# The last superchunk of a macaron block, finished token tile by token tile

## The chip, the cores and the metric

The kernel runs on one core of a Trainium2 chip. The core has TensorE (PE, with its weight loads shown as PEld), VectorE (DVE), ScalarE (ACT), GpSimd (POOL) and the queues that issue transfers, SyncE (SP) and POOL's own. The metric is the device time of one execution in microseconds.

## The reference

The input is x of 8 sequences of 1024 tokens with 256 channels, float32. Three blocks follow each other, each added to its input:

```
x = x + 0.5 * ffn(layernorm(x))
x = x + mamba(layernorm(x))
x = x + 0.5 * ffn(layernorm(x))

ffn(x):    xq = fp4(x);  h = silu(xq @ fp4(w_gate).T) * (xq @ fp4(w_up).T)      # 704 wide
           return fp4(h) @ fp4(w_down).T
fp4(v):    blocks of 16 along the last axis: scale = max(max|v| / 6, 1e-12),
           v / scale rounded to the grid 0, .5, 1, 1.5, 2, 3, 4, 6, times scale
mamba(x):  xi, z = split(norm(x) @ in_proj)            # 512 each
           xi = silu(causal depthwise conv of 4(xi));  dt, B, C = split(xi @ x_proj)
           delta = softplus(dt @ dt_proj + b)
           for each of 16 states n, along time:  h_n = exp(-A_n delta) h_n + delta xi B_n
           y = sum over n of h_n * C_n  +  D * xi
           return (y * silu(z)) @ out_proj
```

## The kernel before

Each sequence is cut into two superchunks of 512 tokens, 16 in all (0 to 15). A superchunk goes through five stages, written as generators: `stage_f1` (first feed-forward), `stage_m1` (up to delta and its product with the convolved input), `stage_z` (the gate silu(z), written to DRAM as `szd`), `scan` (the 16 states) and `stage_out` (gating, out projection, second feed-forward). `spread` gives each yield of each generator a due time, so that stages of neighbouring superchunks are written down interleaved. Inner channels lie on partitions in four chunks (`dc` 0 to 3), tokens along the free axis; the out projection and the feed-forwards work on token tiles of 128 (four in a superchunk).

The order that the program keeps is not the written one. At the end `set_order` builds a graph of all instructions with costs (`price`) and lags, makes eight plans forward and backward over the whole program, and fixes the order of each engine's instructions to the plan with the least estimated end. A change in one place can so move instructions elsewhere.

In `scan`, state k of a superchunk goes through `scan_step` (L802: the recurrence on DVE, one instruction for each inner chunk) and `times_c` (L810: h times C, nearly always on POOL, two inner chunks at a time), and is then added to y in DRAM by a transfer that accumulates (L835, POOL's queue). There are two such sums, for even and odd states. For the last superchunk (`s >= S - KE`, superchunk 15) the last two states, 14 and 15, are not sent to DRAM: `times_c` takes one inner chunk at a time there (state 14 on POOL, state 15 on DVE), and the two h are kept in `last_h`. `load_y` fetches the sum of the other states: one load by SP (L753) and one accumulating load by POOL's queue (L754).

In `stage_out` of the last superchunk, for each inner chunk, DVE adds both kept h to y (L768), the gate's chunk is loaded into `o_sz` (one buffer, L770), and DVE multiplies (L771). Only with all four inner chunks done can a token tile's out projection be complete: four matmuls (L776), which contract over the inner chunks, and the addition to x (L777). The second feed-forward follows: `ln_stats` (bn_stats on DVE, small operations on ACT, a power on POOL), normalization on ACT (L541) into `f_xn`, `quant` (L459 to L469: block maximum on DVE, scale `q_sc` on POOL, reciprocal on DVE, product, square on ACT into PSUM, two rounding passes on DVE, product), transposes on PE (L547), copy to `f_xt` (L549). This is done for two tiles at a time (`XN = 2`). Then for each tile `ffn_h` (gate and up matmuls L559, tanh L562, products L563 and L564 into `f_h`), `quant` of `f_h`, and `ffn_o` (transposes L571 and L575, copies into `f_ht`, down projection L579, addition L580). The products of `quant` of x are on POOL, for `f_h` of the last superchunk's tiles the first is on DVE and the second on POOL. For earlier superchunks both are on POOL, and `f_ht` has one buffer.

PSUM tiles of `stage_out` of the last superchunk are taken in turn from three small pools: `PSM[5] = (1, 0, 1, 0, 2)`, with two, one and one buffers in pools 0, 1 and 2.

Of the kernel before, what the change touches and what calls it, by code (L numbers as in the profile page):

```python
# [20 lines left out]
P = 128  # L21
T = 512
# [14 lines left out]
KS = 1  # L37
KE = 1
# [4 lines left out]
BUFS = {  # L43
    'accd': 4, 'bcol': 2, 'big': 2, 'bu': 8, 'carry': 2, 'cbc': 2, 'cd': 4, 'da': 4, 'delta': 2,
# [3 lines left out]
}  # L48
T_O = 0.1
XN = 2  # L50
QN = 768
DG = 2
HXP = (0, 1, 2, 3)
YG = 2
# [7 lines left out]
ND = DI // P  # L62
# [293 lines left out]
def macaron(ctx: ExitStack, tc: tile.TileContext, x_in, norm_w, norm_b, in_w, conv_w,  # L356
            conv_b, xp_w, dt_w, dt_b, a_log, d_par, out_w, w_gate, w_up, w_down, out):
    nc = tc.nc
    NB, L, _ = x_in.shape
    chunks = []  # L360
    for b in range(NB):
        t = 0
# [24 lines left out]
    sb, psq, psb, dr = Pool(sb), Pool(psq), Pool(psb), Pool(dr)  # L387
    pools = [Pool(q) for q in pools]

    def pst(shape, name):  # L390
        turn[kind[0]] += 1
        i = PSM[kind[0]][turn[kind[0]] % len(PSM[kind[0]])]
        t = pools[i].tile([P, 512], F32, tag=f"ps{i}", name=name)
        n = 1
        for k in shape[1:]:
            n *= k
        v = t[: shape[0], :n]
        if len(shape) == 3:
# [16 lines left out]
    def eng(what):  # L415
        return getattr(nc, ENG[what])
# [9 lines left out]
    outw = cload([P, ND, DM], out_w.rearrange("(c p) n -> p c n", p=P), "outw")  # L426
# [104 lines left out]
        return [(nm[:, i : i + 1], y[:, i : i + 1]) for i in range(nt)]  # L531


    def ffn_x(x4, nt, stats, t0):
        n = min(XN, nt - t0)
        if len(stats) == t0:
            stats += ln_stats(x4, t0, t0 + n, EPS)
        xn = sb.tile([P, XN, DM], F32, tag="xn", bufs=BUFS["xn"], name="f_xn")[:, :n]
        for j in range(n):
            b, r = stats[t0 + j]  # L540
            nc.scalar.activation(xn[:, j, :], x4[:, t0 + j, :], AF.Identity, bias=b, scale=r)  # L541
        quant(xn.rearrange("p a b -> p (a b)"), n * DM, 1e-12, eng('xx'), eng('xq'))
        for j0 in range(0, n, 2):
            pt = pst([P, 2, 2 * P], "f_pt")
            for j in range(2):
                for c in range(2):
                    nc.tensor.transpose(pt[:, c, j * P : (j + 1) * P], xn[:, j0 + j, c * P : (c + 1) * P], ident)  # L547
            xt = sb.tile([P, 2, 2 * P], F32, tag="xt", bufs=BUFS["xt"], name="f_xt")
            nc.scalar.activation(xt, pt, AF.Copy)  # L549
            for j in range(2):  # L550
                yield xt[:, :, j * P : (j + 1) * P]

    def ffn_h(xt, h2):
        for hf in range(2):
# [24 lines left out]
            nc.tensor.matmul(po, ht[:, k, :], wdn[:, k, :], start=(k == 0), stop=(k == NF - 1))  # L579
        nc.vector.scalar_tensor_tensor(x4[:, t, :], po, 0.25, x4[:, t, :], ALU.mult, ALU.add)  # L580

    def ffn(x4, nt, muls, fine):

        stats = [] if fine else ln_stats(x4, 0, nt, EPS)
        yield
        xts = list(ffn_x(x4, nt, stats, 0))
        yield
        hs = []
        hts = [None] * nt
        if fine:  # L590
            hts = []
            for t in range(0, nt, 2):
                two = sb.tile([P, ND * T], F32, tag="h", bufs=BUFS["h"], name="f_ht")[:, : 2 * NF * P]
                two = two.rearrange("p (t k n) -> p t k n", t=2, k=NF)
                hts += [two[:, 0], two[:, 1]]
        for t in range(nt):
            h = sb.tile([P, FF], F32, tag="h2", bufs=BUFS["h2"], name="f_h2")
            ffn_h(xts[t], h)
            yield
            if t + 1 == len(xts) < nt:  # L600
                xts += ffn_x(x4, nt, stats, len(xts))
# [12 lines left out]
    x1d, accd, szd, cd = {}, {}, {}, {}  # L614
    duT, delta, bcol = {}, {}, {}
# [132 lines left out]
    y_of, last_h = {}, {}  # L748
# [8 lines left out]
    def stage_out(s):  # L757
        n = chunks[s][2]
        nt = n // P
        muls = (eng('hx'), eng('hq')) if s < S - ENDV else (nc.vector, nc.vector)  # L760
        x4 = sb.tile([P, NT, DM], F32, tag="x4", bufs=BUFS["x4"], name="x4b")
        nc.sync.dma_start(x4[:, :nt], x1d[s][:, :nt])
        y = y_of.pop(s) if s in y_of else load_y(s)
        yg = 1 if s in last_h else YG
        for dc in range(0, ND, yg):
            if s in last_h:
                for j in range(2):
                    nc.vector.tensor_tensor(y[:, dc, :], y[:, dc, :], last_h[s][j][:, dc, :], ALU.add)  # L768
            sz = sb.tile([P, YG, T], F32, tag="sz", bufs=BUFS["sz"], name="o_sz")[:, :yg, :n]
            nc.sync.dma_start(sz, szd[s][:, dc : dc + yg, :n])  # L770
            (eng('y') if s < S - KE else nc.vector).tensor_tensor(y[:, dc : dc + yg, :], y[:, dc : dc + yg, :], sz, ALU.mult)  # L771
        yield
        for t in range(nt):
            po = pst([P, DM], "o_po")
            for dc in range(ND):
                nc.tensor.matmul(po, y[:, dc, t * P : (t + 1) * P], outw[:, dc, :], start=(dc == 0), stop=(dc == ND - 1))  # L776
# [26 lines left out]
    def times_c(s, k, h, cbc):  # L803
        n = chunks[s][2]
        c_v = CE[S - 1 - s] if S - 1 - s < len(CE) else 0
        cm = 1 if s >= S - KE and k >= NS - 2 else CM
        for dc in range(0, ND, cm):
            hv = h[:, dc : dc + cm, :]
            eng_c = nc.vector if dc < c_v or cm < CM and k % 2 else nc.gpsimd
            eng_c.tensor_tensor(hv, hv, cbc.unsqueeze(1).to_broadcast([P, cm, n]), ALU.mult)  # L810

    def scan(s):
        n = chunks[s][2]
        if chunks[s][1] == 0:

            carry[chunks[s][0]] = sb.tile([P, NS, ND], F32, tag="carry", bufs=BUFS["carry"], name="s_carry")
        for k in range(0, NS, 2):
            cbc = sb.tile([P, 2, T], F32, tag="cbc", bufs=BUFS["cbc"], name="s_cbc")[:, :, :n]
            nc.sync.dma_start(cbc, cd[s][0:1, k * n : (k + 2) * n].rearrange("o (a t) -> o a t", a=2)
                              .partition_broadcast(P))  # L820
            if s >= S - KE and k == NS - 2:
                y_of[s] = load_y(s)
            last = s >= S - KE and k == NS - 2
            for j in range(2):
                h = sb.tile([P, ND, T], F32, tag="h", bufs=BUFS["h"], name="s_h")[:, :, :n]
                scan_step(s, k + j, h)
                if chunks[s][1] + n < L:
                    nc.scalar.activation(carry[chunks[s][0]][:, k + j, :], h[:, :, n - 1], AF.Copy)  # L828
                times_c(s, k + j, h, cbc[:, j, :])
                if last:  # L830
                    last_h.setdefault(s, []).append(h)
                elif k + j == 1:
                    nc.sync.dma_start(accd[s][1, :, :, :n], h)
                else:
                    nc.gpsimd.dma_start(accd[s][j, :, :, :n], h, accum_op=ALU.add)  # L835
                yield
# [12 lines left out]
    t0 = m1 = 0.0  # L849
    for s in range(S):  # L850
# [42 lines left out]
```

## Time and profile before

| | |
|---|---|
| median of three runs | 2534.21 us (2523.82 to 2535.66) |
| the profiled execution | 2536.37 us, span 2534.4 us |
| instructions | 33625 |
| DVE busy | 2184.4 us (86%) |
| POOL busy | 2177.2 us (86%) |
| ACT busy | 2146.9 us (85%) |
| granted TensorE clock, mean | 0.985 |

The page of a profile gives busy times over the span, the span in slices, the transfers, the chain of waits that ended last, and the costliest groups of instructions. In a group's line stands: line of the kernel, engine, operation, output and inputs by their names, shapes, count, busy time and the mean of one in ns, then the idle time before it and what ended that. In a timeline: start and duration in us, then the same, with the idle time in brackets. In the busy times by stretch: the stretch, its length, the busy time of each engine with the number of instructions, the granted clock, the share of the transfer engines and GB/s. The last superchunk's end is short against the span: its last scan instruction ends at 2448.2 of 2534.4 us.

### The profile page before, as it was taken

The numbers are of one execution on the slowest core, as the hardware profiler recorded it, in microseconds if no ns is written. First come the engines' busy times: TensorE is split into PE (matmuls) and PEld (weight loads), VectorE is DVE, ScalarE is ACT, GpSimd is POOL, SyncE is SP. The second block draws the span as 40 slices with busy tenths as digits, with TensorE's granted clock in tenths as the row PEclk, the third lists the DMA queues.
The fourth block names the chain that finished last, engine by engine and source line by source line (L and its number), as shares of the span: only waits on it lengthen the run. The fifth ranks groups of instructions, "written<-read, shape, count | busy, mean of one in ns | idle before, by whom it ended". The sixth has DMA issues, their size and how long they took to land.

```text
span 2534.4 us, 33625 instructions
## 1 busy us (share of the span) xinstructions
PE 2344.9 (93%) x10980; PEld 1591.6 (63%) x10980; DVE 2184.4 (86%) x3082; ACT 2146.9 (85%) x3952; POOL 2177.2 (86%) x1556
## 2 busy tenths in 40 slices
PE   5989898999999999999999999999999999888876
PEld 3555565766666666666666666666666666655544
DVE  7568797998989899898989899898989989878885
ACT  4489787998989988999888989898989988999842
POOL 4359798899989999899998999899997999899952
PEclk9989999999999999999999999999999999999998
DMA  3049779699888988789897998889896988999950
GB/s 90 9 117 207 194 163 223 163 186 238 166 197 195 218 202 189 205 171 239 176 219 173 201 221 176 211 173 221 195 202 181 189 225 175 216 235 211 232 127 17
DMA packets 113647, 465.57 MB, mean 184 GB/s; under 512 B 14592, under 2 KB 32896, under 8 KB 76864
## 3 DMA queue, kind: packets, MB, share of 16 engines
q0 software_dynamic: 36576, 266.35, 56.3%
q1 hardware_dynamic: 76896, 197.08, 24.2%
q8 instruction: 86, 1.41, 0.2%
q14 instruction: 89, 0.73, 0.1%
HBM read 146.19 MB, written 317.19 MB: 183 GB/s over the span
## 4 chain that ended last, share of the span: by engine, by line
POOL 36%; PE 27%; issue 11%; DVE 9%; ACT 9%; DMA 8%; POOLq 0%; SPq 0%; DVEq 0%; ACTq 0%
POOL s_h L810 20%; PE f_pg L559 4%; PE f_pu L559 4%; PE f_po L579 4%; PE s_pb L800 4%; POOL accd L835 4%; DVE s_h L802 4%; DMA accd<-s_h 3%; PE m_pc L682 3%; POOL f_h L462 3%; POOL f_h L469 3%; ACT s_bu L793 2%; ACT s_da L797 2%; POOL f_xn L469 2%; POOL o_y L771 2%
## 5 line engine op out<-in xcount | busy, mean ns | idle before, releaser
L810 POOL TENSOR_TENSOR s_h<-s_h,s_cbc 128x1024 f32<-128x1024 f32 x512 | 1281.8, 2596 | 51.7 <-ACT s_carry L828 27.0
L797 ACT ACTIVATE s_da<-m_delta,an 128x512 f32<-128x512 f32 x1024 | 714.5, 715 | 44.5 <-DVE s_h L802 42.8
L793 ACT ACTIVATE s_bu<-m_duT,m_bc 128x512 f32<-128x512 f32 x1024 | 693.4, 715 | 15.6 <-PE s_pb L800 14.1
L800 PEld LDWEIGHTS s_pb<-ident,s_bu 128*128 128x128 f32 x4096 | 498.0, 142 | 330.2 <-issue 123.4
L800 PE MATMUL s_pb<-ident,s_bu 128*128 128x128 f32 x4096 | 639.2, 277 | 50.9 <-DVE s_h L802 47.4
L802 DVE TENSOR_TENSOR_SCAN s_h<-s_da,s_carry,s_pb 128x512 f32<-128x512 f32 x512 | 636.5, 1265 | 16.5 <-PE s_pb L800 13.3
L802 DVE TENSOR_TENSOR_SCAN s_h<-s_da,s_pb 128x512 f32<-128x512 f32 x512 | 604.4, 1206 | 35.0 <-PE s_pb L800 21.1
L579 PE MATMUL f_po<-wdn,f_ht 128*128 128x256 f32 x1536 | 393.1, 387 | 11.5 <-ACT f_ht L576 6.8
L559 PE MATMUL f_pg<-wg,f_xt 128*128 128x352 f32 x1024 | 370.5, 473 | 13.7 <-ACT f_xt L549 6.2
L559 PE MATMUL f_pu<-wu,f_xt 128*128 128x352 f32 x1024 | 365.6, 468 | 14.1 <-DVE f_h L563 8.4
L579 PEld LDWEIGHTS f_po<-wdn,f_ht 128*128 128x128 f32 x1536 | 276.1, 192 | 73.3 <-ACT f_ht L576 17.0
L835 POOL DMA_DIRECT2D accd<-s_h x238 | 230.7, 969 | 31.8 <-POOL s_h L810 24.1
L559 PEld LDWEIGHTS f_pu<-wu,f_xt 128*128 128x128 f32 x1024 | 182.6, 193 | 115.7 <-issue 34.5
L682 PE MATMUL m_pc<-m_xp,cdg 128*128 128x512 f32 x512 | 252.7, 595 | 2.4 <-ACT m_car L679 2.4
L469 POOL TENSOR_TENSOR f_h<-f_h,q_sc 128x704 f32<-128x704 f32 x128 | 206.5, 1616 | 54.9 <-DVE f_h L468 50.5
L559 PEld LDWEIGHTS f_pg<-wg,f_xt 128*128 128x128 f32 x1024 | 180.3, 195 | 93.4 <-issue 15.1
L462 POOL TENSOR_TENSOR f_h<-f_h,q_rc 128x704 f32<-128x704 f32 x120 | 184.9, 1541 | 22.7 <-DVE q_rc L461 21.9
L563 DVE SCALAR_TENSOR_TENSOR f_h<-f_h,f_pg 128x352 f32<-128x352 f32 x256 | 128.7, 506 | 86.4 <-ACT f_h L562 85.5
L460 POOL TENSOR_SCALAR q_sc<-q_mx 128x44 f32<-128x44 f32 (+2 forms) x198 | 98.0, 497 | 88.5 <-DVE q_mx L459 83.8
L564 DVE TENSOR_TENSOR f_h<-f_h,f_pu 128x352 f32<-128x352 f32 x256 | 129.5, 507 | 41.6 <-PE f_pu L559 39.9
L562 ACT ACTIVATE f_h<-f_pg 128x352 f32<-128x352 f32 x256 | 115.6, 456 | 48.1 <-PE f_pg L559 46.6
L776 PE MATMUL o_po<-outw,o_y 128*128 128x256 f32 x512 | 129.3, 387 | 5.5 <-POOL o_y L771 2.9
(110 smaller groups left out, 3299.6 us busy)
## 6 DMA issues: line engine op xcount, KB each, us to landing
accd<-s_h POOLq DMA_DIRECT2D x238, 1024.0 KB, 9.7
s_cbc<-cd SPq DMA_DIRECT2D x128, 512.0 KB, 5.6
accd<-m_ud SPq DMA_DIRECT2D x64, 256.0 KB, 9.3
accd<-s_h SPq DMA_DIRECT2D x16, 1024.0 KB, 6.8
szd<-m_tz SPq DMA_DIRECT2D x64, 256.0 KB, 6.8
o_y<-accd SPq DMA_DIRECT2D x16, 1024.0 KB, 9.9
o_y<-accd POOLq DMA_DIRECT2D x16, 1024.0 KB, 9.1
o_sz<-szd SPq DMA_DIRECT2D x30, 512.0 KB, 5.1
```

What stands on the lines that cost most here:

```text
L462: mul0.tensor_tensor(vb, vb, rc.unsqueeze(2).to_broadcast([P, g, BLK]), ALU.mult)
L469: mul1.tensor_tensor(vb, vb, sc.unsqueeze(2).to_broadcast([P, g, BLK]), ALU.mult)
L559: nc.tensor.matmul(dst, xt[:, c, :], w[:, c, hf * FH : (hf + 1) * FH], start=(c == 0), stop=(c == 1))
L564: nc.vector.tensor_tensor(hh, hh, pu, ALU.mult)
L579: nc.tensor.matmul(po, ht[:, k, :], wdn[:, k, :], start=(k == 0), stop=(k == NF - 1))
L682: nc.tensor.matmul(pc, cdg[:, dc, k, :], xp[:, k : k + n], start=(k == 0), stop=(k == KC - 1))
L793: nc.scalar.activation(b, duT[s][t], AF.Copy, scale=bcol[s][:, t, k : k + 1])
L797: nc.scalar.activation(da, delta[s][dc], AF.Exp, scale=an[:, dc, k : k + 1])
L800: nc.tensor.transpose(pb[:, t * P : (t + 1) * P], bu[t][:, dc * P : (dc + 1) * P], ident)
L802: nc.vector.tensor_tensor_scan(h[:, dc, :], da, pb, init, ALU.mult, ALU.add)
L810: eng_c.tensor_tensor(hv, hv, cbc.unsqueeze(1).to_broadcast([P, cm, n]), ALU.mult)
L835: nc.gpsimd.dma_start(accd[s][j, :, :, :n], h, accum_op=ALU.add)
```

## The change

For the last superchunk alone (`end`), four things change.

- The product of state 14 with C goes to POOL in two instructions of two inner chunks each. The product of state 15 with C is no longer made in `scan`; its C row is kept beside h.
- The gate is loaded by one transfer into a buffer of the `delta` tag. State 14's product is added to y by POOL, two inner chunks at a time, for all 512 tokens.
- In the loop over token tiles, for the tile's 128 tokens and all four inner chunks at once: state 15 times C (DVE in tiles 0 and 2, POOL in 1 and 3), its addition to y on DVE, the gating on DVE, then the four matmuls of the out projection and the addition to x as before.
- The second feed-forward prepares x one tile at a time (`XL = 1`) instead of two: statistics, normalization, quantization, transposes and copy.

The first superchunk keeps two tiles at a time (`XF = 2`). New lines shift the line numbers: the recurrence is L814, the products with C L822 and L849, the additions of state 14 L770, of state 15 L784, the gating L785, the out projection L788.

```diff
+XF = 2
+XL = 1
...
-    def ffn_x(x4, nt, stats, t0):
-        n = min(XN, nt - t0)
+    def ffn_x(x4, nt, stats, t0, n=XN):
...
-        for j0 in range(0, n, 2):
-            pt = pst([P, 2, 2 * P], "f_pt")
-            for j in range(2):
-                for c in range(2):
-                    nc.tensor.transpose(pt[:, c, j * P : (j + 1) * P], xn[:, j0 + j, c * P : (c + 1) * P], ident)
-            xt = sb.tile([P, 2, 2 * P], F32, tag="xt", bufs=BUFS["xt"], name="f_xt")
-            nc.scalar.activation(xt, pt, AF.Copy)
-            for j in range(2):
-                yield xt[:, :, j * P : (j + 1) * P]
+        pt = pst([P, 2, n * P], "f_pt")
+        for j in range(n):
+            for c in range(2):
+                nc.tensor.transpose(pt[:, c, j * P : (j + 1) * P], xn[:, j, c * P : (c + 1) * P], ident)
+        xt = sb.tile([P, 2, 2 * P], F32, tag="xt", bufs=BUFS["xt"], name="f_xt")[:, :, : n * P]
+        nc.scalar.activation(xt, pt, AF.Copy)
+        for j in range(n):
+            yield xt[:, :, j * P : (j + 1) * P]
...
-        yield from ffn(x4, nt, (eng('hx'), eng('hq')), s < KS)
+        yield from ffn(x4, nt, (eng('hx'), eng('hq')), s < KS, XF if s < KS else XN)
...
+        end = s in last_h
...
-        yg = 1 if s in last_h else YG
-        for dc in range(0, ND, yg):
-            if s in last_h:
-                for j in range(2):
-                    nc.vector.tensor_tensor(y[:, dc, :], y[:, dc, :], last_h[s][j][:, dc, :], ALU.add)
-            sz = sb.tile([P, YG, T], F32, tag="sz", bufs=BUFS["sz"], name="o_sz")[:, :yg, :n]
-            nc.sync.dma_start(sz, szd[s][:, dc : dc + yg, :n])
-            (eng('y') if s < S - KE else nc.vector).tensor_tensor(y[:, dc : dc + yg, :], y[:, dc : dc + yg, :], sz, ALU.mult)
+        if end:
+            sz = sb.tile([P, ND, T], F32, tag="delta", bufs=BUFS["delta"], name="o_sz")[:, :, :n]
+            nc.sync.dma_start(sz, szd[s][:, :, :n])
+            (h0, _), (h1, c1) = last_h[s]
+            for dc in range(0, ND, 2):
+                nc.gpsimd.tensor_tensor(y[:, dc : dc + 2, :], y[:, dc : dc + 2, :], h0[:, dc : dc + 2, :], ALU.add)
+        else:
...
         for t in range(nt):
+            ts = slice(t * P, (t + 1) * P)
+            if end:
+
+                hv, yv = h1[:, :, ts], y[:, :, ts]
+                (nc.gpsimd if t % 2 else nc.vector).tensor_tensor(
+                    hv, hv, c1[:, ts].unsqueeze(1).to_broadcast([P, ND, P]), ALU.mult)
+                nc.vector.tensor_tensor(yv, yv, hv, ALU.add)
+                nc.vector.tensor_tensor(yv, yv, sz[:, :, ts], ALU.mult)
             po = pst([P, DM], "o_po")
...
-        yield from ffn(x4, nt, muls, s >= S - KE)
+        yield from ffn(x4, nt, muls, end, XL if end else XN)
...
-                times_c(s, k + j, h, cbc[:, j, :])
                 if last:
-                    last_h.setdefault(s, []).append(h)
+                    last_h.setdefault(s, []).append((h, cbc[:, j, :]))
+                else:
+                    times_c(s, k + j, h, cbc[:, j, :])
+                if last:
+                    if j == 0:
+                        for dc in range(0, ND, 2):
+                            hv = h[:, dc : dc + 2, :]
+                            nc.gpsimd.tensor_tensor(hv, hv, cbc[:, j, :].unsqueeze(1).to_broadcast([P, 2, n]), ALU.mult)
                 elif k + j == 1:
```

More of the change, by code (lines that the diff above doesn't have):

```diff
@@ L580, in ffn_o, with ffn @@
         nc.vector.scalar_tensor_tensor(x4[:, t, :], po, 0.25, x4[:, t, :], ALU.mult, ALU.add)
-    def ffn(x4, nt, muls, fine):
+    def ffn(x4, nt, muls, fine, xn=XN):
         stats = [] if fine else ln_stats(x4, 0, nt, EPS)
         yield
-        xts = list(ffn_x(x4, nt, stats, 0))
+        xts = list(ffn_x(x4, nt, stats, 0, xn))
         yield
@@ L600, in ffn @@
             if t + 1 == len(xts) < nt:
-                xts += ffn_x(x4, nt, stats, len(xts))
+                xts += ffn_x(x4, nt, stats, len(xts), xn)
                 yield
@@ L763, in stage_out @@
         y = y_of.pop(s) if s in y_of else load_y(s)
-        yg = 1 if s in last_h else YG
-        for dc in range(0, ND, yg):
-            if s in last_h:
-                for j in range(2):
-                    nc.vector.tensor_tensor(y[:, dc, :], y[:, dc, :], last_h[s][j][:, dc, :], ALU.add)
-            sz = sb.tile([P, YG, T], F32, tag="sz", bufs=BUFS["sz"], name="o_sz")[:, :yg, :n]
-            nc.sync.dma_start(sz, szd[s][:, dc : dc + yg, :n])
-            (eng('y') if s < S - KE else nc.vector).tensor_tensor(y[:, dc : dc + yg, :], y[:, dc : dc + yg, :], sz, ALU.mult)
+        if end:
[5 more added lines that the diff above has]
+        else:
+            for dc in range(0, ND, YG):
+                sz = sb.tile([P, YG, T], F32, tag="sz", bufs=BUFS["sz"], name="o_sz")[:, :, :n]
+                nc.sync.dma_start(sz, szd[s][:, dc : dc + YG, :n])
+                (eng('y') if s < S - KE else nc.vector).tensor_tensor(y[:, dc : dc + YG, :], y[:, dc : dc + YG, :], sz, ALU.mult)
         yield
         for t in range(nt):
+            ts = slice(t * P, (t + 1) * P)
[5 more added lines that the diff above has]
+                nc.vector.tensor_tensor(yv, yv, sz[:, :, ts], ALU.mult)
             po = pst([P, DM], "o_po")
             for dc in range(ND):
-                nc.tensor.matmul(po, y[:, dc, t * P : (t + 1) * P], outw[:, dc, :], start=(dc == 0), stop=(dc == ND - 1))
+                nc.tensor.matmul(po, y[:, dc, ts], outw[:, dc, :], start=(dc == 0), stop=(dc == ND - 1))
             nc.vector.tensor_tensor(x4[:, t, :], x4[:, t, :], po, ALU.add)
         yield
-        yield from ffn(x4, nt, muls, s >= S - KE)
+        yield from ffn(x4, nt, muls, end, XL if end else XN)
         nc.sync.dma_start(tok(out, s), x4[:, :nt])
```

## The prediction

> **What bounds the kernel now.** I read the page first, then the chain of waits over the last 155 us, the busy times by stretch there, the timeline where the chain showed a wait, and the groups and tiles for durations. The page gives the whole:
>
> ```profile
> span 2534.4 us, 33625 instructions
> PE 2344.9 (93%) x10980; PEld 1591.6 (63%) x10980; DVE 2184.4 (86%) x3082; ACT 2146.9 (85%) x3952; POOL 2177.2 (86%) x1556
> ```
>
> All engines are 85 to 93% busy, so the body is a balanced pipeline and no single engine there can give much. The change rewrites only the end. The chain of waits shows what sets it (start, duration, what):
>
> ```profile
> 2441.08 7.95 DMA o_y<-accd
> 2449.05 0.69 DVE o_y L768
> ...
> 2467.52 2.87 PE f_po L579 x12
> 2470.41 0.44 DVE x4b L580
> 2470.89 2.01 PE o_po L776 x8
> ...
> 2483.20 1.13 PE f_pt L547 x4
> 2484.36 0.60 ACT f_xt L549
> 2485.01 2.71 PE f_pg L559 x4
> ```
>
> The load of y ends the wait at 2449.05, the down projections of superchunk 14 end at 2470.4, the out projection follows, and 12 us later the first gate matmul runs. The same by stretch (PE, PEld, DVE, ACT, POOL busy, then the granted clock):
>
> ```profile
> 2441.00:2470.85 29.85, 22.41 (x90) 14.91 (x88) 22.47 (x33) 4.63 (x9) 8.10 (x6) 0.94 0.26 61
> 2470.85:2485.00 14.15, 5.54 (x22) 3.98 (x22) 5.88 (x16) 3.98 (x10) 4.24 (x7) 0.74 0.11 37
> 2485.00:2524.00 39.00, 32.89 (x118) 21.59 (x119) 26.14 (x42) 10.51 (x20) 8.02 (x10) 0.92 0.00 1
> ```
>
> In the middle stretch no engine is half busy: it is pure latency, paid for two tiles together. That is what can be won. In the first, POOL is idle for 22 of 30 us while DVE is three quarters busy.
>
> **The change part by part.** The order in which the changed program's instructions stand shows more than the diff: the planner also moves superchunk 14's feed-forward ahead of the last scans, and puts the load of y on POOL behind the second half of state 14's product. I follow that order with durations of this trace. Anchor: the end of state 13's scans, 2426.35 before.
>
> *Scans.* By this point DVE now runs four more f_h operations (4 x 0.51) and one less z gating (0.68): 2427.7. From there to the end of state 14's scans DVE has 4 scans (5.1), four f_h quantization passes (3.5), three gate or up products (1.5) and 2.8 of small ones: 12.9, so 2440.6. POOL's 1024-wide product takes 2.5, so with 0.3 of lags the load of y issues at 2443.4 instead of 2441.1 and, at 7.95, lands at 2451.4: 2.3 later.
>
> *Sum of the two last states.* Removed: eight DVE additions (L768) and four DVE products, one in each inner chunk. Added: on POOL two additions of 1024 elements, on DVE per tile an addition and a gating and in every other tile a product, all 512 elements. The nearest rows, POOL's 1024-wide o_y gating and DVE's additions and products (min/median/max ns):
>
> ```profile
> L771 POOL TENSOR_TENSOR o_y<-o_y,o_sz x30: 2351/2378/2968, 304.8 to 2368.8; 128x1024 f32<-128x1024 f32 x30
> L768 DVE TENSOR_TENSOR o_y<-o_y,s_h x8: 621/687/1873, 2449.1 to 2463.9; 128x512 f32<-128x512 f32 x8
> L810 DVE TENSOR_TENSOR s_h<-s_h,s_cbc x4: 680/682/1864, 2441.1 to 2456.4; 128x512 f32<-128x512 f32 x4
> ```
>
> POOL is held by the quantization of the fourth tile of superchunk 14: sc behind the issue of the load (2445.1), reciprocal on DVE (2445.6), product (2447.3), ACT (2448.2), two DVE passes (2450.1), product (2452.0). So its two additions end at 2457.0. DVE has finished everything else and waits there; nothing useful is queued behind it. Then addition and gating: 1.4. The maxima of 1.87 and 1.86 are the price of POOL beside DVE:
>
> ```profile
> 2456.07 1.64 POOL L462 TENSOR_TENSOR f_h<-f_h,q_rc 128x704 f32<-128x704 f32 x1 [0.88 <-DVE q_rc L461]
> 2456.39 1.86 DVE L810 TENSOR_TENSOR s_h<-s_h,s_cbc 128x512 f32<-128x512 f32 x1
> ```
>
> The DVE product ended at 2458.25, one plain duration after POOL's 2457.71. Tile 1's product starts on POOL just as tile 0's addition becomes ready on DVE, so I charge 1.86 - 0.68 = 1.2 there: tile 0 of y is ready at 2459.7, where all of y was ready at 2467.3. [...]
>
> *The loads of sz.* Four loads become one of 1024 KB into a buffer of their own, which takes away the 1.57 us wait at 2466.6. It needs all four z writes, the last of which now follows state 14's scans (2441.3): plus 0.3 to issue, 6.0 to 6.8 for szd to land, 6.2 to 9.9 for 1024 KB (rows of o_y by SP) gives 2453.8 to 2458.3. It is wanted at 2459.0: hidden under POOL's additions, by 0.7 at worst; with another wait ahead of it, 1 late. I take 0.
>
> *Out projection.* On PE it stands behind the last down projection of superchunk 14. That chain of three (5.8 us each, one buffer) ended at 2470.4 because it was queued behind an up projection that waited 2.9 for DVE. Now its last part starts when POOL is done, 2452, and ends at 2457.7. Tile 0's eight matmul records (2.01) run from 2459.8, its addition ends at 2462.3. Before, the pair was complete at 2473.36: 11.1 earlier.
>
> *Normalization and quantization of x.* From there to the first gate matmul the pair took 2485.01 - 2473.36 = 11.65. One tile takes less: one bn_stats (0.42), one aggregate (0.17) and one normalization (0.59) fall out; reduce 0.32 and reciprocal 0.1; POOL's two products from 1.06 to 0.61 each (slope between 512 and 704 elements), 0.9; the two ACT passes 0.21 each; the two DVE passes 0.27 each; half of the transposes, 0.56. Sum 4.0, leaving 7.65. Against it other tiles' work now stands between: tile 3's product on POOL ahead of sc (1.4) and 1.5 of DVE ahead of the reciprocal, partly under each other: 2.3. So 9.95, and the first gate matmul starts at 2472.2: 12.8 earlier.
>
> *The split itself.* Four small quantizations replace two: DVE pays the fixed part of four operations twice more. From 352 (517 ns) to 704 (892 ns) elements the fixed part is 142 ns, so 8 x 0.14 = 1.1, plus 0.8 of tile 3's addition and statistics now inside the stretch that begins at 2488.25 (first f_h product) and ends at 2523.85. DVE is idle for 9.5 of those 35.6 us (26.1 busy), and I charge 0. If that cover is gone (tile 3's gate matmuls stand behind the first down projection on PE, as before), it costs up to 3. [...]
>
> *Clock.* The granted clock is 0.74 in the latency stretch; the first four gate matmul records take 2.71 and a group of up matmuls at 2498.09 again 2.71, against 1.35 for others. PE will idle less before them. Bounds 0 and 2.7; I take 1.4.
>
> Sum: 12.8 + 1.4 = 14.2 us, of which the last stretch after 2524 keeps its length. The profiled execution took 2536.37 (span plus 1.97), so 2522.2 on its scale; the median of the runs is 2.2 lower, which gives **2520.0 us**, 0.56% faster. A difference under 0.5% (12.7 us) is about what a measurement of this kernel can't tell from none.
>
> **Rivals.** *The gain shrinks* to 5 to 11 us: second port block 1.2, sz 1, cover gone 3, no clock gain 1.4, and the load of y landing at the 9.9 of its slower rows (2). All together 8.6, so 2528.6; about half, 2524. For it: DVE's order in the stretch is dense. Against: they don't add on one path, since sz and y end before POOL does.
>
> *Slower, by the replanned body.* The planner works on the whole program, and from an eighth of it on the order differs by some places on every engine. The body is the same work planned differently in each superchunk, so its spread prices an order. The loads of y on POOL, every second one, are one sequence apart:
>
> ```profile
> 1032.87 0.89 POOL L754 DMA_DIRECT2D o_y<-accd  x1
> 1321.49 0.91 POOL L754 DMA_DIRECT2D o_y<-accd  x1 [0.28 <-issue]
> 1612.74 0.92 POOL L754 DMA_DIRECT2D o_y<-accd  x1
> 1912.66 0.90 POOL L754 DMA_DIRECT2D o_y<-accd  x1
> ```
>
> That is 288.6, 291.3 and 299.9 us per pair; with the pairs from 445.46, 743.28 and to 2209.10 (297.8, 289.6, 296.4) the mean is 293.9. If all six pairs became like the slowest, 6 x 6.0 = 36 us would be lost and the time would be 2556. It decides when the body loses over 26.9 us, 4.5 per pair. Against it: most instructions move by two or three places only, and spreads should average out; a typical change is 4 per pair in either direction, about 10 over six.
>
> *The same with the other sign*: a body better by 10 on top of the gain gives 2510.
>
> *It doesn't do what it says*: PE still runs three tiles' out projections before the first transposes. That costs nothing as long as tile 2 of y (2465) is ready before tile 0's quantization ends (2471); if PE waits for tile 2 instead, 2 to 4 us are lost, within the first rival.
>
> **How the numbers follow.** The sum as it stands, 0.62: of it 0.48 beats 12.7 us and 0.14 doesn't, as its distance to that bound is small. The shrunk gain 0.17, within 0.5%. The body better 0.10, faster. The body worse by over 26.9 us 0.11, slower. So faster 0.58, same 0.31, slower 0.11. Range: the gain between 6 (the first rival whole) and 18 (no port block, the whole 2.7 of the clock, 0.8 instead of 2.3 between), with the body 11 better beside the large one or 9 worse beside the small one: 2505 to 2537. It leaves out the slow body and the best of the good one. The sum's own range is 2514 to 2526.
>
> **What would show it.** In the changed profile: the load of y on POOL issued some 2.3 us after its old place relative to state 13, and an addition pair on POOL of 2.4 each right after a f_h product; tile 0's addition of the out projection about 9 us, the first gate matmul about 13 us earlier relative to the last scans; less than 12 us from that addition to the gate matmul; one DVE addition stretched to some 1.9; the stretch from the first f_h product to the last quantization pass still near 36. The prediction is wrong if that stretch grows by 3 or more, if DVE waits for sz, or if the last scan itself ends 10 us off from 2448 to 2451, which would be the body.

## The result, and the profile after

The changed kernel takes 2551.26 us (median, 2550.14 to 2555.81). Run beside it, the kernel before took 2533.2, so the ratio is 1.0073 with an interval of 1.0050 to 1.0095: some 18 us slower, where 14 faster was forecast. The profiled execution took 2550.14 us. The span and the busy times from the page of the changed kernel:

```profile
span 2548.4 us, 33646 instructions
PE 2355.4 (92%) x10980; PEld 1601.8 (63%) x10980; DVE 2182.5 (86%) x3084; ACT 2147.4 (84%) x3960; POOL 2186.8 (86%) x1568
```

DVE and ACT do the same work to within 2 us, PE and POOL about 10 us more, and the span grew by 14.0. The chain of waits of the changed kernel, over the end (start, duration, what):

```profile
2465.93 4.54 PE f_po L579 x12
...
2479.11 4.54 PE f_po L579 x12
...
2484.22 1.98 PE o_po L788 x8
...
2496.31 1.19 PE f_pg L559 x2
```

The links are those that the prediction named: last down projection of superchunk 14, out projection, first gate matmul. But all of it is some 11 to 13 us later than before, where the first gate matmul was forecast 13 earlier. The busy times by stretch of the changed kernel (PE, PEld, DVE, ACT, POOL, granted clock, share of the transfer engines, GB/s), cut at the load of y, at the addition of tile 0, at the first gate matmul and after the last pass:

```profile
2465.90:2486.20 20.30, 16.86 (x64) 12.56 (x64) 9.96 (x12) 2.72 (x5) 9.97 (x7) 0.83 0.48 123
2486.20:2496.30 10.10, 4.42 (x18) 3.08 (x18) 8.11 (x20) 2.56 (x8) 4.79 (x8) 1.00 0.04 14
2496.30:2538.00 41.70, 36.26 (x129) 24.55 (x130) 28.60 (x53) 12.73 (x30) 12.61 (x20) 0.88 0.00 0
```

From the load of y to the first gate matmul it is 30.4 us (43.9 before), and from the load to the end of the span 82.5 (93.3 before). So the end did get shorter, by 10.8. The loss arose before the load. The accumulating loads of y on POOL, in the timeline of the changed kernel, of the superchunks shown for the kernel before, and of the last one:

```profile
1035.11 0.94 POOL L754 DMA_DIRECT2D o_y<-accd  x1
1331.38 0.92 POOL L754 DMA_DIRECT2D o_y<-accd  x1 [0.66 <-DMA o_y<-accd]
1624.05 0.92 POOL L754 DMA_DIRECT2D o_y<-accd  x1
1917.46 0.91 POOL L754 DMA_DIRECT2D o_y<-accd  x1
2465.94 0.92 POOL L754 DMA_DIRECT2D o_y<-accd  x1 [1.01 <-DMA o_y<-accd]
```

They come 2.2, 9.9, 11.3 and 4.8 us later than before, and the last one 24.9. No instruction in these stretches was edited; the planner, which planned the whole program anew, put them in another order.

### The profile page after: what moved, and what is told of

It is laid out like the page before. It is cut to its first block, busy times and chain, and to the rows that moved or that the text cites. A ratio compares the mean times of both kernels' runs of the same rounds, so it can differ in the third digit from the quotient of the medians.

```text
span 2548.4 us, 33646 instructions
## 1 busy us (share of the span) xinstructions
PE 2355.4 (92%) x10980; PEld 1601.8 (63%) x10980; DVE 2182.5 (86%) x3084; ACT 2147.4 (84%) x3960; POOL 2186.8 (86%) x1568
## 4 chain that ended last, share of the span: by engine, by line
POOL 37%; PE 26%; issue 12%; DMA 9%; DVE 8%; ACT 8%; POOLq 0%; SPq 0%; DVEq 0%; ACTq 0%
POOL s_h L822 21%; PE f_pg L559 5%; PE f_pu L559 4%; PE f_po L579 4%; PE s_pb L812 4%; POOL accd L853 4%; DVE s_h L814 3%; DMA accd<-s_h 3%; POOL f_h L464 3%; PE m_pc L682 2%; POOL f_h L471 2%; DMA accd<-m_ud 2%; POOL f_xn L471 2%; ACT s_bu L805 1%; PE o_po L788 1%
## 5 line engine op out<-in xcount | busy, mean ns | idle before, releaser
L822 POOL TENSOR_TENSOR s_h<-s_h,s_cbc 128x1024 f32<-128x1024 f32 x508 | 1274.0, 2594 | 60.1 <-ACT s_carry L840 36.4
L814 DVE TENSOR_TENSOR_SCAN s_h<-s_da,s_carry,s_pb 128x512 f32<-128x512 f32 x512 | 634.7, 1262 | 23.0 <-PE s_pb L812 18.1
L814 DVE TENSOR_TENSOR_SCAN s_h<-s_da,s_pb 128x512 f32<-128x512 f32 x512 | 604.3, 1205 | 38.5 <-PE s_pb L812 31.3
L462 POOL TENSOR_SCALAR q_sc<-q_mx 128x44 f32<-128x44 f32 (+3 forms) x200 | 99.2, 496 | 78.9 <-DVE q_mx L461 73.9
L788 PE MATMUL o_po<-outw,o_y 128*128 128x256 f32 x512 | 132.0, 394 | 10.2 <-DVE o_y L785 3.5
```

The source lines that it names most:

```text
L788: nc.tensor.matmul(po, y[:, dc, ts], outw[:, dc, :], start=(dc == 0), stop=(dc == ND - 1))
L814: nc.vector.tensor_tensor_scan(h[:, dc, :], da, pb, init, ALU.mult, ALU.add)
```

## The experiments

Theory A: the order that the new plan gave to the unchanged body costs the time, and the edits themselves gain. Theory B: the edits cost the time. Two instants cut each profile in three: superchunk 13's load of y on POOL, the last load of y, and the end of the span. Each instant and length is read from one profile. Kernels that share an order reach the same instant up to 14 us apart (more on that below), so instants have to be read with care; how far the length to the end differs between executions of one kernel, no run here shows. All kernels, in us (each ratio is to runs of the kernel before made beside it):

| kernel | median | ratio to before, interval | load of 13 at | to last load | to the end |
|---|---|---|---|---|---|
| before | 2532.0 to 2535.0 | | 2209.1 | 232.0 | 93.3 |
| changed | 2551.3 | 1.0073 (1.0050 to 1.0095) | 2213.9 | 252.0 | 82.5 |
| e1 changed, body in the order of before | 2542.0 | 1.0044 (1.0029 to 1.0058) | 2204.4 | 236.7 | 98.7 |
| e2 before, body in the changed order | 2555.0 | 1.0096 (1.0078 to 1.0115) | 2215.5 | 249.8 | 85.9 |
| e3 before, x one tile at a time | 2540.3 | 1.0021 (1.0004 to 1.0037) | 2203.8 | 232.9 | 90.9 |
| e4 changed, x two tiles at a time | 2560.3 | 1.0111 (1.0095 to 1.0126) | 2219.1 | 251.5 | 88.7 |
| e5 changed, order of before to load of 13 | 2524.9 | 0.9967 (0.9951 to 0.9982) | 2195.4 | 239.0 | 82.2 |
| e6 before, planned anew | 2539.0 | 1.0024 (1.0009 to 1.0039) | 2197.0 | 250.2 | 90.5 |
| e7 before, planned anew, second number | 2523.2 | 0.9962 (0.9946 to 0.9979) | 2178.6 | 245.5 | 93.6 |
| e8 changed, planned anew | 2530.5 | 0.9988 (0.9972 to 1.0005) | 2201.9 | 244.4 | 84.7 |
| e9 changed, all common instructions in the order of before | 2528.6 | 0.9987 (0.9971 to 1.0003) | 2201.2 | 232.9 | 92.6 |
| e10 changed, planned anew, second number | 2521.6 | 0.9968 (0.9947 to 0.9989) | 2193.5 | 244.7 | 83.0 |
| e11 e1 with PE's waits filled | 2528.9 | 0.9975 (0.9962 to 0.9988) | 2204.3 | 234.4 | 90.4 |
| e12 before, own order to load of 13 | 2535.7 | 1.0004 (0.9989 to 1.0020) | 2203.3 | 234.3 | 97.6 |
| e13 before, changed order, then own | 2556.2 | 1.0090 (1.0062 to 1.0118) | 2218.4 | 240.1 | 91.0 |
| e14 before, own order, then changed | 2538.1 | 1.0014 (0.9998 to 1.0030) | 2202.7 | 246.3 | 86.8 |

**Which part of it: order or edits.** An order is kept by giving the planner's graph one more edge from each listed instruction to the one ahead of it on its engine; `kept()` lists them by their place in the written program, which is the same in both kernels up to the last superchunk's end:

```diff
+        last = {}
+        for x in kept():
+            if self.eng[x] in last:
+                dep(x, last[self.eng[x]], False)
+            last[self.eng[x]] = x
```

Run e1 is the changed kernel with the list from the plan of before, up to the store of the last superchunk's state 12; e2 is the kernel before with the list from the changed plan, up to the same store.

> The changed kernel, with one thing added to the planner's graph: up to the accumulating store of state 12 of the last superchunk, each engine's instructions keep the order that they have in the kernel before; the end is planned freely. Theory A (the loss of the change is the order of the body, which the planner rearranged): the load of y on POOL issues at 2441 to 2446 as before, the end after it takes 82 to 85 us as in the changed kernel, and the time is 2518 to 2527 us, faster than before by 6 to 15. Theory B (the loss comes with the change's own instructions near the end: the state 14 product and the load of y behind POOL's work, the gate's load in the delta buffer): the load of y still issues 15 us or more late, and the time is 2540 to 2552.

> The kernel before, with the order of the body up to the store of state 12 of the last superchunk taken from the changed kernel; the end is the old one and planned freely. Theory A (the order of the body is the loss): the load of y issues at 2458 to 2466, the end takes 90 to 94 us as before, and the time is 2550 to 2560 us, slower than the changed kernel. Theory B (the change's own instructions near the end are the loss): 2530 to 2538, as before.

e2 has none of the edits and is as slow as the changed kernel: the order of the body is enough for the whole loss. e1 gets its last load of y at 2441.0, as before, so the other half of theory A holds too: without the new order the edits don't delay the body. But its end is 98.7 long, longer than that of before, and its time falls into the range of theory B, neither of which theory A foresaw. e11 below takes that up. e2's end is 85.9 instead of the 90 to 94 expected: the order alone shortens it.

**Each edit alone.** e3 leaves the sum over states as it was and only prepares x one tile at a time; e4 is the changed kernel with

```diff
-XL = 1
+XL = 2
```

> Of the change only the quantization of x tile by tile; the end of the sum, the gating and the out projection as before; everything planned freely. Its body gets another order again. Theory A: the end from the load of y on is 3 to 5 us shorter than before (88 to 90 us), and the load of y issues anywhere from 2432 to 2466, which decides the time: 2522 to 2556. Theory B: the load of y issues at 2439 to 2443 and the time is 2527 to 2533.

> The change without its part on x: two tiles at a time are quantized, as before; the end of the sum, gating and out projection go by token tile. Its instructions stand in the changed kernel's order all through the body. Theory A (order of the body): the load of y issues at 2463 to 2468 as in the changed kernel, the end is 85 to 89 us, and the time 2552 to 2558. Theory B (the change's own instructions are the loss): the same late load, as all of these are in it; the two theories differ here only in that A expects nothing from the part on x but the end's 3 to 5 us.

e4 has the changed kernel's order in the body, and loses in the body what that loses (last load 2470.6, somewhat more than expected, as is its time). Its end is 88.7, against 82.5 with x one tile at a time and 93.3 with neither; e3's is 90.9. Against before, the sum alone is thus 4.6 shorter, x alone 2.4, the two together 10.8. But these kernels differ in order too, and e2 shows that an order alone can shorten the end. At one order of the body, that of the changed kernel, x one tile at a time takes 6.2 off the end (88.7 to 82.5), and the time, by the two ratios, is 0.38% less; the sum alone leaves an end 2.8 longer than that of e2 (85.9), which has neither edit. That the edit of x gains is shown for that order; that the edit of the sum gains by itself is not. e3's median beside its profile (2529.7) says little: its runs lie from 2526.9 to 2546.7.

**Another draw of the plan.** e6 and e8 change one lag in the planner's model, which no instruction depends on, in the kernel before and in the changed one; e7 and e10 another (ScalarE to TensorE, 171 for 170):

```diff
-(ET.DVE, ET.PE): 130
+(ET.DVE, ET.PE): 131
```

> The kernel before with one number of the planner changed that says nothing of the change: the assumed lag from DVE to PE is 131 instead of 130. The instructions are the same; their order is not. If an order is worth as much as the spread of superchunks in the trace of before says (4 us per pair), the time is 2515 to 2550, and the load of y issues 5 to 15 us away from 2441 in either direction. If an order is worth little, 2530 to 2535 and 2439 to 2443.

> The changed kernel with the same neutral number, 131 instead of 130. If its loss is an accident of its plan, the time falls to 2520 to 2540. If it belongs to how the new end draws superchunk 14 forward, which this plan does as well, the interval from the load of y of superchunk 13 to the last one stays 245 to 255 us (before: 232) and the time is 2545 to 2560.

> The kernel before with one neutral number of its planner changed: the assumed lag from ScalarE to TensorE is 171 instead of 170. The program computes the same with the same instructions, only their order differs. Theory A (the order of the body that a re-plan draws is worth tens of us either way): the time lies anywhere from 2525 to 2560, and with it the instant of superchunk 13's load of y, 2195 to 2220; the last stretch from the last load of y to the end stays near 90 to 99 us. Theory B (the order is worth little and the changed kernel's loss is from its own edits): 2528 to 2538.

> The changed kernel with the same neutral number, 171 instead of 170. Theory A: the time lies anywhere from 2520 to 2555, and the difference to the changed kernel is one of the body: the last load of y moves with the time, while the stretch from it to the end stays near 82 to 88 us. It should be shorter than that of the kernel before with the same number, by 3 to 11 us. Theory B: 2546 to 2556 as the changed kernel itself.

With the same instructions, the changed kernel takes 2551.3, 2530.5 and 2521.6, the kernel before 2533, 2539.0 and 2523.2. The end hardly takes part: 82.5, 84.7 and 83.0 against 93.3, 90.5 and 93.6. It is the last load of y that moves: 2465.9, 2446.3 and 2438.3 against 2441.1, 2447.2 and 2424.1. Theory B is dead: its 2546 to 2556 for e10 missed by 24 us. Theory A's own ranges for e7 were too narrow: its time is 2 us below them and its load of superchunk 13, at 2178.6, 16 us. And the 232 us between the two loads, which e8's expectation took as what the kernel before has, is the exception: planned anew, that kernel takes 250.2 and 245.5, the changed one 244.4 and 244.7, so a long stretch there does not come with the edits. The end is shorter by 9.1 on the mean of three and the last load of y later by 12.7. Three draws that spread over 23 and 28 us cannot tell that 12.7 from nothing.

**One order for both.** e5 keeps the list of before up to superchunk 13's load of y in the changed kernel and plans freely behind it; e12 does the same to the kernel before. e9 keeps all 16981 instructions that both kernels have in common in the order of before.

> The changed kernel; the order of the kernel before is kept only up to the load of y of superchunk 13 (the one at 2209 us), and superchunks 14 and 15 are planned freely. Theory A1 (the planner, to shorten its new end, pulls superchunk 14's feed-forward ahead of superchunk 15's scans, and pays for it there): the last load of y issues at 2455 to 2464 instead of 2441, the end after it takes 82 to 86 us, and the time is 2540 to 2550. Theory A2 (the loss is an accident of the order in the body before that): the last load issues at 2438 to 2446 and the time is 2520 to 2530.

> The kernel before, with its own order kept up to superchunk 13's load of y and planned anew behind it: the control of the run in which the changed kernel was kept in that order up to the same place and took 2524.9. If that gain is from the change's own end, this one takes 2530 to 2536 with a last stretch of 90 to 93 us. If it is from planning the last two superchunks anew, this one takes 2522 to 2528 and its last load of y comes before 2437.

> The changed kernel in which all instructions that both kernels write down in the same order up to state 14's product keep the order of the kernel before; only what follows is placed freely. So superchunk 14's feed-forward is not drawn forward. Theory A1: the load of y issues at 2441 to 2444; superchunk 14's last down projection still ends near 2470 and holds the new out projection, so that the early y is worth nothing; the single tile gains 2 us on the way to the first gate matmul and the stretch of four tiles loses 1.5: 2529 to 2535. By the recorded prediction, whose gain came with y: 2518 to 2526.

Given one order ahead of superchunk 13, the changed kernel takes 0.9967 and the kernel before 1.0004 of the same reference: 0.37% or 9.4 us between them, though each was compared with its own set of runs of before. The time of e12 came within its first range, so planning the end anew does not make e5's gain; its own end, at 97.6, is worse than the 90 to 93 expected. In e9, where superchunk 14's feed-forward has to stand where it stood, the end is 92.6, and the gain is gone from it; its load of y, at 2434.1, is 7 us earlier than expected, which one profile can't explain. Ends of 82 to 85 us were seen only with the edits *and* superchunk 14's work in a new place. The times alone don't show that the gain needs both: e9's 0.9987 and e5's 0.9967 have intervals that overlap.

**Why e1's end was long.** In e1 PE is busy for only 2.0 of the 5 us from 2440 to 2445. Its timeline shows the wait, and the busy times by stretch the clock behind it:

```profile
2445.58 2.71 PE L829 MATMUL f_pu<-wu,f_xt 128*128 128x352 f32 x4 [3.50 <-DVE f_h L833]
```

```profile
2455.00:2460.00 5.00, 3.08 (x9) 1.77 (x9) 3.76 (x5) 0.98 (x2) 2.99 (x3) 0.50 0.00 0
```

The clock granted is 0.50 in this stretch and in the two of 5 us ahead of it, 15 us in all. e11 keeps e1's order on every engine and fills PE's waits with 55 transposes that nobody reads:

```diff
+    for n in FILL:
+        w = psb.tile([P, T], F32, tag="psb", name="w_fill")
+        for _ in range(n):
+            nc.tensor.transpose(w[:, :P], ident, ident)
```

> The kernel of the first experiment (changed kernel, body in the order of before) with its exact order on every engine, and 55 more transposes of 128x128 of the identity placed on TensorE in the waits of superchunk 14's last tiles, into a PSUM tile that nobody reads. It adds work and leaves nothing out. If idle time of TensorE lowers the granted clock there (0.50 from 2445 to 2460 in the first experiment), the clock stays above 0.8, the gate and up groups fall from 2.71 to about 1.45 us and the down products from 5.46 and 4.54 to about 2.9; some 8.6 us are saved, the last stretch is about 90 and the time about 2533. If the clock does not hang on that idle time, the groups stay at 2.7 and the time at 2538 to 2548.

The same stretch of e11, and then one down projection in PE's timeline of e1 and of e11:

```profile
2455.00:2460.00 5.00, 4.00 (x24) 3.10 (x23) 2.21 (x3) 1.55 (x3) 0.24 (x1) 1.00 0.00 0
```

```profile
2459.14 5.46 PE L849 MATMUL f_po<-wdn,f_ht 128*128 128x256 f32 x12 [0.47 <-ACT f_ht L846]
```

```profile
2452.32 2.86 PE L857 MATMUL f_po<-wdn,f_ht 128*128 128x256 f32 x12 [0.25 <-ACT f_ht L854]
```

The clock stays at 1.00 from 2440 to 2465, the group takes 2.86 instead of 5.46, the end is 8.3 shorter (expected: 8.6) and the median 13 us lower, more than the end accounts for. That idle time on PE lowers the clock here (0.50 from 2445 to 2460 with the waits, 1.00 with them filled), and that this made e1's end long, is shown by taking it away. A wait of 3.50 us stands ahead of the first slow group; why the clock then stayed at 0.50 until 2460, with PE busy for 3.08 to 3.89 of each 5 us, no run shows. The clock was as low without so long a wait: in the changed kernel it is 0.50 from 2466 to 2468, with PE busy for 1.40 of the 3 us ahead of that and no wait over 1.00 us in the 6 us ahead. Filled, e1's edits at the order of before leave an end of 90.4, 2.9 shorter than before. But before was not filled: its clock was 0.74 from 2470.85 to 2485, and what filling would take off its end, no run shows.

**Where in the order.** By the two profiles alone, the changed kernel is 4.8 us late at superchunk 13 and 24.9 late at the last load, which points at the last two superchunks. e13 and e14 are the kernel before with one order ahead of superchunk 13's load and the other behind it (a change of the list only).

> The kernel before, in the order of the changed kernel up to superchunk 13's load of y, and in its own order behind that up to the accumulating store of the last superchunk's state 12. If the loss lies in the order of the last two superchunks, this run is freed of it: the stretch from superchunk 13's load to the last load of y takes 230 to 239 us and the time is 2528 to 2542. If the loss lies before that place, the stretch still starts late and the time is 2545 to 2560. If the two halves only fit together as they were planned (the order behind the seam needs the order ahead of it), the stretch is over 240 although it has the order of before, and both runs of this pair are slow.

> The kernel before, in its own order up to superchunk 13's load of y, and in the order of the changed kernel behind that up to the same store. If the loss lies in the order of the last two superchunks, this run has it: the stretch from superchunk 13's load to the last load of y takes 245 to 253 us, the DMA engines' share in it falls to about 0.90 from 0.96, and the time is 2543 to 2558. If it lies before that place, the stretch takes 230 to 239 us and the time is 2522 to 2536.

Busy times by stretch from superchunk 13's load to superchunk 14's, and on to the last load, of the kernel before, then of the changed kernel, then of e14:

```profile
2209.10:2334.20 125.10, 109.21 (x504) 67.90 (x504) 101.02 (x121) 116.87 (x214) 114.84 (x71) 1.00 0.95 221
2334.20:2441.10 106.90, 84.84 (x406) 57.96 (x406) 95.98 (x117) 83.22 (x139) 98.95 (x65) 0.94 0.96 215
```

```profile
2213.90:2351.60 137.70, 120.77 (x540) 77.58 (x539) 106.47 (x130) 121.09 (x223) 116.67 (x73) 0.95 0.88 203
2351.60:2465.90 114.30, 92.00 (x432) 61.63 (x432) 102.73 (x122) 90.21 (x152) 103.82 (x65) 0.93 0.91 200
```

```profile
2202.65:2334.90 132.25, 113.12 (x495) 72.76 (x495) 97.72 (x121) 111.11 (x205) 112.49 (x70) 0.95 0.91 208
2334.90:2449.00 114.10, 94.24 (x438) 62.75 (x438) 103.92 (x123) 89.82 (x152) 103.28 (x67) 0.91 0.92 203
```

e14 has the long stretch (246.3, as expected for the order of the last superchunks) but not the long time that went with it (2538.1, where 2543 to 2558 was expected); e13 is slow although its stretch, 240.1, is only 8 us longer than that of before. So the loss lies on both sides, and most of what stays in the time lies ahead of superchunk 13. The reading by two profiles was misled: the profile of before is the latest of seven that have its order up to there (2195.4 to 2209.1, mean 2202.9; e1, e5, e9, e11, e12 and e14 are the others), while four with the changed order (the changed kernel, e2, e4 and e13) lie from 2213.9 to 2219.1, mean 2216.7. In the traces, DVE's instructions up to that load stand in one order in all seven, and in one other order in all four. That is 13.8 us ahead of superchunk 13.

Behind it the stretch is 12 to 20 longer in the changed order. There the transfer engines are 95% busy before: share times length makes 221 us of transfer time before, 225 in the changed kernel and in e14. The transfers are nearly the same (50.70 and 50.83 MB), and in the longer stretch they are busy for a smaller share of it (0.88 to 0.92, against 0.95 and 0.96). But not all of that is lost. The changed order also does 972 matmul records there where that of before does 910, of which 43 had been done earlier in the order of before (so at superchunk 13's load the changed kernel is behind in work too, not only in time) and 19 came after it (232 left for the end against 251). Part of the longer stretch is thus work that has to be caught up or is brought forward, and e14's shorter end (86.8) gives 6.5 of its 14.3 back.

What stays open: which instructions of the order cost the 14 us ahead of superchunk 13, and why e13 is, by its median, some 12 us slower than its three stretches' usual lengths add up to (2216.7 + 234 + 93.3 = 2544).

**A version that beats both.** e5 (0.9967) and e10 (0.9968) have the change and are faster than either kernel, but e7, with no edit at all, is as fast (0.9962). What the change takes off the end (9.1 us on the mean of three pairs, 3.4 at one order of the body, worked out below) is no more than what one number in the planner does: 2533 to 2523 in the kernel before, 2551 to 2522 in the changed one.

## Why the prediction was wrong

**The step that failed is the body.** The sum took the body as unchanged, at nothing, and gave a slower one, as a rival, 0.11. The runs showed that the new order of the unchanged instructions is enough for the loss: e2, without any of the edits, takes 2555.0. State 13's last scan ended at 2426.35 before and at 2448.91 after (DVE's timeline of before, then of after):

```profile
2425.07 1.28 DVE L802 TENSOR_TENSOR_SCAN s_h<-s_da,s_carry,s_pb 128x512 f32<-128x512 f32 x1 [1.39 <-PE s_pb L800]
```

```profile
2447.64 1.27 DVE L814 TENSOR_TENSOR_SCAN s_h<-s_da,s_carry,s_pb 128x512 f32<-128x512 f32 x1
```

That is 22.6 us of body, from which the end's own gain of 8.6 is taken off to make the 14.0 between the spans. The rival was named rightly, as was its sign in the view to look at (the last scan, 10 us off), but its usual price, about 10 us, and its chance were too small, for two reasons. The pairs of superchunks used for it ended with superchunk 13's load, so that the last two superchunks, where the change's neighbours are, were not priced at all; the body lost another 20 us there between the two profiles. And the argument that most instructions move by only two or three places and that spreads average out is refuted by e6, e7, e8 and e10, where the last load of y moved by up to 28 us with every instruction the same. With re-plans this wide the chance of a slower result could not be 0.11.

**Its threshold was off as well.** 26.9 us to be lost counted on a gain of 14.2. With the 8.6 that came, 21.3 is enough.

**The end, term by term,** measured from the end of state 13's scans, which takes the body out:

- The load of y: 2.3 later was forecast, and 17.0 after against 14.7 before is 2.3.
- Its landing: forecast 7.95, and the wait for it on POOL ended at 2476.59, 10.65 after the issue. POOL was to be held by the quantization until later than that; it waited 1.13 for the transfer. The 7.95 was that of one load; the page of before has 9.1 as the median of all 16. Tile 0 of y is so ready at 34.8 instead of 33.35.
- POOL beside DVE: one block of 1.2 was charged. Timeline of the changed kernel, POOL, then DVE:

```profile
2476.59 4.64 POOL L770 TENSOR_TENSOR o_y<-o_y,s_h 128x1024 f32<-128x1024 f32 x2 [1.13 <-DMA o_y<-accd]
2481.19 1.26 POOL L782 TENSOR_TENSOR s_h<-s_h,s_cbc 128x512 f32<-128x512 f32 x1
```

```profile
2481.27 1.74 DVE L784 TENSOR_TENSOR o_y<-o_y,s_h 128x512 f32<-128x512 f32 x1 [4.59 <-POOL o_y L770]
```

  The addition beside POOL's product takes 1.74, ending with it to within 0.6 (forecast 1.86); the other three take 0.68 to 0.69. The "second port block" of 1.2, a term of the first rival, is shown by no run, nor is a port between the two engines: tile 3's product ran from 2489.57 to 2490.83, when no addition to y ran on DVE, only a block maximum (0.42) and an addition to x (0.41), against 0.41 for tile 1's maximum and 0.42 for tile 0's addition.
- The load of sz, issued at 2466.8, delayed nothing: taken at 0, and 0.
- The down projections of superchunk 14 ended later than forecast: two of three groups took 4.54 instead of 2.86, 3.4 us. The clock granted was 0.50 from 2466.00 to 2468.00 and 0.64 from 2479.10 to 2481.00, in these two groups, and 1.00 in the one between them; the working had priced no clock there. Their last addition is at 2483.69, so the out projection (2484.22) started half a microsecond after y was ready. Tile 0's addition so ends at 37.7 instead of 35.95. The 11.1 credited to this step came as 9.3.
- From that addition to the first gate matmul: 9.95 forecast, 9.7 measured. The gate starts 11.3 earlier than before, where 12.8 was forecast.
- The clock: a credit of 1.4 was taken. The gate matmuls ran at 1.19 and 1.31 for two, at a clock of 0.59 from 2496 to 2500, with four of tile 3's eight out projection matmuls (1.91) between them on PE, and the first f_h product came 4.54 after the gate instead of 3.24: a loss of 1.3, and 2.7 away from the sum. The working had not seen that part of tile 3's out projection would stand between the gate matmuls.
- The split's cover: 35.6 forecast to stay, 37.1 measured; 1.5 of the 3 that an uncovered split was to cost. Whether the cover or the clock (0.50 from 2515 to 2520) took them is not shown.

Together 1.5 + 2.7 + 1.5 = 5.7 of the 14.2 are missing, and to within 0.1 that leaves the 8.6 which the profiles show. That is in the first rival's range (5 to 11), right for the end and wrong for the total; of its terms the late landing of y and the missing clock credit came true, and neither a second block beside POOL nor sz did.

**What the 11.1 was made of.** The step let the out projection start earlier because the planner had drawn superchunk 14's feed-forward ahead of the last scans. That is no gain of the edits: the kernel before in that order has an end of 85.9 (e2) and 86.8 (e14), 6.5 to 7.4 shorter, and pays for it with a longer stretch ahead. At the changed kernel's order of the body the edits are worth 3.4 (82.5 against e2's 85.9). At the order of before they lose 5.4 (e1's 98.7 against 93.3); with PE's waits filled as well they gain 2.9 (e11), against a kernel that was not filled. I counted the early start as gain and the body, where the work went, as unchanged.

## What to carry to other kernels

Where a planner orders the whole program, price a small edit at its end against the spread of re-plans, and measure that spread by changing a number that no instruction depends on before believing a difference of one per cent. A shorter tail that rests on work drawn ahead of its first instant is no gain until the stretch ahead of that instant has been charged for it. Profiles of one order differed here by up to 13.7 us at an instant of 2200, so a place of loss read from one profile each is a guess until the order is swapped at that place.

## What was not expected of the hardware

- A wait of 3.5 us on TensorE was followed by 15 us at a granted clock of 0.50, with gate, up and down groups at nearly twice their time (2.71 for 1.45, 5.46 for 2.86); 55 transposes that nobody reads (20 of them took 2.35 us), in waits that nobody used, held it at 1.00 and saved 8.3 us of the end.
- One order gave superchunk 13's load of y at instants from 2195.4 to 2209.1 in seven profiles of kernels that keep the same order up to there: 0.6% with nothing changed ahead of that instant.
